# A graph layer kernel on Trainium2: preparation steps divided, edge counts moved beside the keys, two phases given other groups

## The chip, the cores and the metric

The kernel runs on one core of a Trainium2 chip. The metric is the time of one execution on the device in microseconds (us). The engines of the core are named as in the profile: PE (TensorE, matmuls; PEld is its weight load), DVE (VectorE), ACT (ScalarE), POOL (GpSimd) and SP (SyncE, which here issues nearly all DMAs). Each engine works through its own instructions in their order and waits for other engines by semaphores.

## The reference, cut to what matters

There are 32 independent graphs (B) of 512 nodes (N) with 128 features (D). One entry in sixteen of the adjacency matrix, and its diagonal, is not zero.

```python
# layer 0
adj = adj + eye(N)
d = adj.sum(axis=2) ** -0.5
x = layernorm(x + (d[:, :, None] * adj * d[:, None, :]) @ (x @ w0) + b0)
# layer 1, once for each pair (i, j)
pre = (x @ W1[:D])[:, None, :, :] + (x @ W1[D:])[:, :, None, :] + b1
msg = gelu(layernorm(pre, g1, be1))
agg = einsum("bijo,bij->bio", msg, adjacency)
updated = layernorm(concatenate([x, agg]) @ W2 + b2, g2, be2)
x = layernorm(x + updated)
```

The messages of layer 1 cost most. The kernel computes them only for pairs that are edges.

## The kernel before

**Slots and groups.** The 512 nodes of a graph lie in four chunks of 128 (C = 4). For each of the 16 pairs of chunks, the kernel makes a list of the edges of each node: eight slots with the first eight edges, one extra slot for the diagonal pairs of chunks, and two slots of "shared places" for what is left of crowded pairs. A slot has four groups (one for each chunk of receivers), the extra slot has one, so a graph has 8 x 4 + 1 + 2 x 4 = 41 groups, numbered 0 to 40: groups 0 to 31 are the eight slots, 32 is the extra slot (slot 8), 33 to 40 are the shared ones (slots 9 and 10). Over 32 graphs there are 1312 groups.

**The main loop** (in `sparse_path`) runs over the groups in order. One iteration n does this:

- `fetch` (for a slot that begins soon): `gathered`, five groups ahead, reads the slot's list of node numbers from DRAM, spread to all partitions (`raw`, L677). `gathers`, three groups ahead, makes a one-hot matrix of it on DVE (`s`, L687) and has SP transpose it by DMA (`mt`, L689). `deviations` reads three rows per term of the standard deviations (`sd_rows`, L705).
- `pairs(n)` on PE: 16 bf16 matmuls (L724, L725) into a PSUM tile `u`, which has three buffers. In the shared slots, four f32 matmuls (L720) come first; these need `sj` and `ac`, not the one-hot.
- `pass_on`: `aggregate(n-3)` on PE (L772), `sums(n-1)` on DVE (`u_sb`, L734, not in shared slots), `weights(n-1)` on POOL (`sw`, four buffers, L749), `messages(n-2)` on ACT (`m`, L763).
- one step of `finish` of the previous graph, if it is open: the last matmul (`pu`), `u` with its bias (L641), two normalizations, the output.
- `prepare(n)`: some steps of the work that makes ready a later graph or the later slots of this one.

**The preparation** is written as generators. Each `yield` ends a step. The table `plan` gives for each phase the number of steps, and from which group to which (relative to group 0 of its graph) they are spread evenly. So `layer0` of the next graph runs beside groups 0 to 21 of this one, `lists` and `parts` beside 22 to 32, `factors` beside 33 to 37, `more` from group 31 to group 7 of its own graph, and `shared` beside groups 8 to 27.

What these phases do, as far as it is touched here:

- `layer0`: loads `xs` and `a_nat` (1 MB), transposes the adjacency on PE into four banks (L249), and for each bank ACT sums a row (`copied` with `accum_out=deg`, L260) and copies the bank to `a_t` (L261). One DVE instruction makes `mask` (L263) of all four. ACT counts the edges by four sums over `mask` (`counted`, L293). POOL makes the inverse root of the degrees and `xb`. ACT makes `s` and `own_s` (L297, L302). PE multiplies (`pconv`, L311, two halves), DVE makes `y` (L318), a normalization gives `x1` (L208), and PE and ACT turn it (`x1t`, L328). Then `pat`, `pct`, squares and sums on PE and ACT, and at last the `key`s: for each of four q, a matmul `pv` (L365) and two DVE instructions (L361, L362) that read `mask`.
- `lists`: 16 times the eight largest keys and their places on DVE (L399, L400), which ACT casts (`idx_h`, L404), PE turns (`pidx`, L408) and SP writes to DRAM (`idx_d`).
- `more`: 32 steps of three DVE instructions (L455, L457, L458): take out the eight found, find the next eight, and their places. They write into spare columns of `a_t`.
- `shared`: a block of five DVE instructions (L469 to L479), a small count over partitions (`count_h`, `po`, `first`), 16 DVE comparisons (`ended`, L512), eight matmuls and comparisons (`pj` L526, `sj` L522), 16 pairs of matmuls with a copy by ACT (`pl` L537, `sent` L533), the choice of the node numbers in two halves (`chosen`, `picked`, L553, L561), then casts, matmuls and the writes of the extra and shared lists to DRAM (`idx_ds` from `idx_rs`, L582, L386; `sd_ds`). Slots 8, 9 and 10 read those lists.

**Order.** For ACT, POOL and DVE the main loop is under `manual_schedule`: their instructions stand as the code issues them. PE's and SP's instructions are put in order by the framework's planner, which uses its own estimates. Pools with one buffer (`raw` of a width, `mask`, `a_nat`) make a later writer wait for the last reader of what was there.

Of the kernel before, what the change touches and what calls it, by code (L numbers as in the profile page):

```python
# [8 lines left out]
F32 = mybir.dt.float32  # L9
BF16 = mybir.dt.bfloat16  # L10
I32 = mybir.dt.int32
U32 = mybir.dt.uint32
AF = mybir.ActivationFunctionType
ALU = mybir.AluOpType
# [4 lines left out]
P = 128  # L19
# [8 lines left out]
def bcast(ap, n):  # L28

    return ap.unsqueeze(1).to_broadcast([ap.shape[0], n, ap.shape[-1]])  # L30
# [16 lines left out]
def sparse_path(ctx, tc, x, adj, w0, b0, w1, b1, g1, be1, w2, b2, g2, be2, out, most):  # L47
# [21 lines left out]
    nc = tc.nc  # L69
    B, N, D = x.shape  # L70
    C = N // P
# [3 lines left out]
    node = ctx.enter_context(tc.tile_pool(name="node", bufs=1))  # L75
# [67 lines left out]
    rows = {}  # L143
# [72 lines left out]
    def transposed(src, key):  # L216

        pt = bank(f"pt_{key}")
        for c in range(C):
            nc.tensor.transpose(pt[:, c * P : (c + 1) * P], src[:, c, :], ident)  # L220
        return pt
# [3 lines left out]
    def pause(n):  # L225

        for _ in range(n):
            yield

    def layer0(b):  # L230
# [11 lines left out]
        st["edges"] = edges  # L242
        deg = small.tile([P, C], F32, tag="deg", name=f"deg_{b}")
        mask = big.tile([P, C, N], BF16, tag="mask", name=f"mask_{b}")
        px = transposed(xs, f"x_{b}")
        for mc in range(C):
            pt = bank(f"pa_{b}_{mc}")
            for c in range(C):
                nc.tensor.transpose(  # L249
                    pt[:, c * P : (c + 1) * P], a_nat[:, c, mc * P : (mc + 1) * P], ident  # L250
                )
            if mc == 2:
                psup = bank(f"psup_{b}")
                for c in range(C):
                    nc.tensor.matmul(
                        psup[:, c * P : (c + 1) * P], x_t[:, c * P : (c + 1) * P], w0_sb, start=True, stop=True
                    )
            yield
            copied = small.tile([P, N], BF16, tag="copied", name=f"copied_{b}_{mc}", bufs=1)
            nc.scalar.activation(copied, a_nat[:, mc, :], AF.Copy, accum_out=deg[:, mc : mc + 1])  # L260
            nc.scalar.copy(a_t[:, mc, :, :P], pt.rearrange("p (c i) -> p c i", i=P))  # L261
            if mc == C - 1:
                nc.vector.tensor_scalar(  # L263
                    mask.rearrange("p q (c i) -> p (q c) i", i=P),
                    a_t.rearrange("p q c w -> p (q c) w")[:, :, :P],
                    0.0,
                    1.0,
                    ALU.is_equal,
                    ALU.subtract,
                )  # L270
            if mc == 0:
                x_t = node.tile([P, N], F32, tag="t0", name=f"x_t_{b}")
                nc.scalar.copy(x_t, px)
        yield from pause(2)

        deg1 = small.tile([P, C], F32, tag="deg1", name=f"deg1_{b}")
        nc.gpsimd.tensor_scalar(deg1, deg, 1.0, None, ALU.add)
# [7 lines left out]
        nc.gpsimd.tensor_sub(dinv, rdeg, none)  # L285
        dinv2 = small.tile([P, C], F32, tag="dinv2", name=f"dinv2_{b}", bufs=1)
        nc.gpsimd.tensor_tensor(dinv2, dinv, dinv, ALU.mult)
        xb = node.tile([P, C, D], F32, tag="t2", name=f"xb_{b}")
        nc.gpsimd.tensor_tensor(xb, xs, bcast(rows["b0"], C), ALU.add)

        for q in range(C):
            copied = small.tile([P, N], BF16, tag="copied", name=f"counted_{b}_{q}", bufs=1)
            nc.scalar.activation(copied, mask[:, q, :], AF.Copy, accum_out=edges[:, q : q + 1])  # L293

        s = node.tile([P, C, D], F32, tag="t1", name=f"s_{b}")
        for c in range(C):
# [11 lines left out]
        for c in range(C):  # L308
# [4 lines left out]
                )  # L313
            if c % 2:
                yield
        y = node.tile([P, C, D], F32, tag="t3", name=f"y_{b}")
        for c in range(C):
            nc.vector.scalar_tensor_tensor(  # L318
                y[:, c, :], pt[:, c * P : (c + 1) * P], dinv[:, c : c + 1], xb[:, c, :], ALU.mult, ALU.add
            )  # L320
        x1 = node.tile([P, C, D], F32, tag="x1", name=f"x1_{b}", bufs=3)
        yield from layernorm(y, x1, f"l0_{b}")
        st["x1"] = x1
# [33 lines left out]
        key = big.tile([P, C, N], F32, tag="key", name=f"key_{b}")  # L357
        for q in range(C + 1):
            if q:
                here = key[:, q - 1, :]  # L360
                nc.vector.scalar_tensor_tensor(here, pt, a_sum[:, q - 1 : q], c_sum, ALU.add, ALU.add)  # L361
                nc.vector.scalar_tensor_tensor(here, here, -TINY, mask[:, q - 1, :], ALU.min, ALU.mult)  # L362
            if q < C:
                pt = bank(f"pv_{b}_{q}")
                nc.tensor.matmul(pt, at2[:, q * P : (q + 1) * P], ct, start=True, stop=True)  # L365
            yield
# [94 lines left out]
    def shared(b):  # L461
# [7 lines left out]
        nc.vector.scalar_tensor_tensor(over, var, 0.0, sharing, ALU.is_gt, ALU.mult)  # L469
        count = small.tile([P, C * C], F32, tag="count", name=f"count_{b}", bufs=1)  # L470
        nc.vector.tensor_reduce(count, over, AX.X, ALU.add)

        here = small.tile([P, C * C, SLOTS], F32, tag="here", name=f"here_{b}", bufs=1)
        nc.vector.tensor_scalar(here, st["top"], 0.0, None, ALU.is_gt)
# [56 lines left out]
        for n in range(C * C + 1):  # L531
            if n:
                nc.scalar.copy(sent[:, n - 1], pt[:, : SHARED * WIDE].rearrange("p (k w) -> p k w", w=WIDE))  # L533
            if n < C * C:
                pt = bank(f"pl_{b}_{n}")
                for k in range(SHARED):
                    nc.tensor.matmul(  # L537
                        pt[:, k * WIDE : (k + 1) * WIDE],
                        sj[:, n, k * P : (k + 1) * P],
                        at[:, n, :],  # L540
                        start=True,
                        stop=True,
                    )
            if n % 2:
                yield
        yield from pause(3)

        n_r = SHARED * C * C
        chosen = big.tile([P, 2, SHARED, C * C, MORE], F32, tag="mask", name=f"chosen_{b}")
# [80 lines left out]
    def finish(b):  # L630

        st = state.pop(b)
        aggt = st["aggt"]
        pt = bank(f"pu_{b}")
        for c in range(C):
            o, here = pt[:, c * P : (c + 1) * P], slice(c * P, (c + 1) * P)
            nc.tensor.matmul(o, st["x1t"][:, here], w2_sb[:, 0, :], start=True, stop=False)
            nc.tensor.matmul(o, aggt[:, here], w2_sb[:, 1, :], start=False, stop=True)
        yield
        u = node.tile([P, C, D], F32, tag="f0", name=f"u_{b}")  # L640
        nc.vector.tensor_tensor(u, pt.rearrange("p (c d) -> p c d", d=D), bcast(rows["b2"], C), ALU.add)  # L641
        yield
        un = node.tile([P, C, D], F32, tag="f1", name=f"un_{b}")
        yield from layernorm(u, un, f"l1_{b}")
        nc.gpsimd.tensor_tensor(un, un, bcast(rows["g2"], C), ALU.mult)
        yield
        nc.gpsimd.tensor_tensor(un, un, bcast(rows["be2"], C), ALU.add)
        yield
        nc.gpsimd.tensor_tensor(un, un, st["x1"], ALU.add)
        yield  # L650
        o_sb = node.tile([P, C, D], F32, tag="f0", name=f"o_sb_{b}")
        yield from layernorm(un, o_sb, f"l2_{b}")
        yield
        nc.sync.dma_start(out[b].rearrange("(c p) d -> p c d", p=P), o_sb)
# [129 lines left out]
    def advance(gens, steps=1):  # L784
# [12 lines left out]

    n_groups = len(order)
    plan = [
        (layer0, 26, -n_groups, -19),  # L800
        (lists, 21, -19, -8),
        (parts, 7, -19, -10),
        (factors, 7, -8, -3),
        (more, 33, -10, 8),
        (shared, 45, 8, 28),
    ]
    running = {}

# [337 lines left out]
```

## Time and profile before

| | |
|---|---|
| Median of the runs shown | 4013.91 us (three runs, 4012.98 to 4014.3) |
| The profiled execution | 4011.64 us |
| Its span, first to last instruction | 4009.9 us |
| Mean granted clock of PE | 0.985 |
| DMA packets, bytes | 902107, 419.99 MB (105 GB/s in the mean) |
| PE's two largest groups | L772 agg, 1495.7 us; L724 u, 1433.9 us |
| DVE's largest | L734 u_sb, 713.4 us in 1056; L687 s, 421.5 us in 352 |
| ACT's largest | L763 m, 1294.0 us and 288.3 us |
| POOL's largest | L749 sw, 1216.8 us and 296.4 us |

The busy time of an engine is that in which at least one of its instructions is at work. A matmul of f32 operands is shown as two instructions. The number behind "x" is a count, that in brackets at the end of a timeline row is the idle time before, with what ended it. A timeline's columns are: start in us from the span's start, length in us, engine, line, operation, output <- inputs, shapes, count.

### The profile page before, as it was taken

The numbers are of one execution on the slowest core, as the hardware profiler recorded it, in microseconds if no ns is written. First come the engines' busy times: TensorE is split into PE (matmuls) and PEld (weight loads), VectorE is DVE, ScalarE is ACT, GpSimd is POOL, SyncE is SP. The second block draws the span as 40 slices with busy tenths as digits, with TensorE's granted clock in tenths as the row PEclk, the third lists the DMA queues.
The fourth block names the chain that finished last, engine by engine and source line by source line (L and its number), as shares of the span: only waits on it lengthen the run. The fifth ranks groups of instructions, "written<-read, shape, count | busy, mean of one in ns | idle before, by whom it ended". The sixth has DMA issues, their size and how long they took to land. (4 is left out here: it accounts for less than half of the span.)

```text
span 4009.9 us, 108439 instructions
## 1 busy us (share of the span) xinstructions
PE 3766.3 (94%) x39744; PEld 3510.3 (88%) x39744; DVE 3263.9 (81%) x10645; ACT 2791.9 (70%) x8321; POOL 2225.5 (55%) x2526
## 2 busy tenths in 40 slices
PE   5999999999999999999999999999999999999997
PEld 5988889888899888898888998888998889888887
DVE  6888888888887888888888888888888888788892
ACT  4777677676776766776767767667767677676664
POOL 4555565555655555655556555556555565555554
PEclk7999999999999999999999999999999999999998
DMA  3444444444444444444444444444444444444442
GB/s 85 107 109 106 114 101 106 107 107 105 113 102 106 108 106 110 106 106 106 107 105 113 102 106 108 106 112 104 106 105 108 105 108 106 108 107 105 98 105 56
DMA packets 902107, 419.99 MB, mean 105 GB/s; under 512 B 724304, under 2 KB 882192, under 8 KB 901568
## 3 DMA queue, kind: packets, MB, share of 16 engines
q1 hardware_dynamic: 901344, 412.52, 44.1%
q8 instruction: 317, 5.19, 0.5%
q14 instruction: 222, 1.82, 0.1%
q0 software_dynamic: 224, 0.46, 0.1%
HBM read 227.15 MB, written 13.76 MB: 60 GB/s over the span
## 5 line engine op out<-in xcount | busy, mean ns | idle before, releaser
L749 POOL TENSOR_TENSOR sw<-mt,a_t 128x512 f32<-128x512 bf16 x1056 | 1216.8, 1164 | 918.1 <-PE agg L772 764.0
L772 PE MATMUL agg<-sw,m 128*128 128x128 f32 x10496 | 1495.7, 285 | 76.2 <-POOL sw L749 46.1
L724 PE MATMUL u<-c,s 128*128 128x128 bf16 x15744 | 1433.9, 220 | 84.0 <-DVE u_sb L734 80.3
L763 ACT ACTIVATE m<-u_sb,r 128x128 f32<-128x128 f32 x4096 | 1294.0, 395 | 142.3 <-DVE u_sb L734 57.8
L772 PEld LDWEIGHTS agg<-sw,m 128*128 128x128 f32 x10496 | 1304.5, 192 | 94.2 <-POOL sw L749 51.3
L724 PEld LDWEIGHTS <-s 128*128 128x128 bf16 x15744 | 1191.2, 98 | 115.0 <-issue 40.9
L725 PE MATMUL u<-be,sd_rows 128*128 128x128 bf16 x5248 | 1148.6, 220 | 20.7 <-DMA sd_rows<-sd_ds 14.6
L734 DVE TENSOR_TENSOR u_sb<-u,ac 128x512 f32<-128x512 f32 x1056 | 713.4, 676 | 200.6 <-PE u L725 177.1
L725 PEld LDWEIGHTS <-sd_rows 128*128 128x128 bf16 x5248 | 512.7, 98 | 30.7 <-issue 20.0
L763 ACT ACTIVATE m<-u,r_s 128x128 f32<-128x128 f32 x1024 | 288.3, 363 | 251.6 <-PE agg L772 247.4
L533 ACT COPY sent<-pl 128x352 f32<-128x352 f32 x512 | 228.9, 447 | 315.9 <-PE pl L537 278.8
L687 DVE TENSOR_SCALAR s<-raw,node_p 128x2052 bf16<-128x2052 bf16 (+1 forms) x352 | 421.5, 1197 | 20.6 <-DMA raw<-idx_ds 11.9
L720 PE MATMUL u<-ac,sj 128*128 128x128 f32 x2048 | 437.8, 296 | 0.0
L749 POOL TENSOR_TENSOR sw<-mt,sent 128x512 f32<-128x512 bf16 x256 | 296.4, 1163 | 229.0 <-PE agg L772 176.2
L537 PEld LDWEIGHTS pl<-a_t,sj 128*128 128x128 f32 x2048 | 316.2, 191 | 60.7 <-issue 59.2
L457 DVE MAX8 a_t<-key 128x8 f32<-128x128 f32 x1024 | 301.2, 294 | 34.5
L537 PE MATMUL pl<-a_t,sj 128*128 128x176 f32 x2048 | 327.4, 313 | 1.3 <-POOL a_t L505 1.3
L522 DVE TENSOR_SCALAR sj<-pj,node_p 128x512 f32<-128x512 f32 x256 | 187.7, 745 | 153.8 <-PE pj L526 153.8
L720 PEld LDWEIGHTS u<-ac,sj 128*128 128x128 f32 x2048 | 310.0, 192 | 0.4
L458 DVE FIND_INDEX8 idx_m<-a_t,key 128x8 uint32<-128x128 f32 x1024 | 291.4, 285 | 0.0
L311 PEld LDWEIGHTS pconv<-s,a_t 128*128 128x128 f32 x1024 | 141.3, 214 | 57.1 <-ACT s L297 55.4
L361 DVE SCALAR_TENSOR_TENSOR key<-pv,a_sum,c_sum 128x512 f32<-128x512 f32 x128 | 95.7, 748 | 108.3 <-PE pv L365 108.3
(178 smaller groups left out, 4788.8 us busy)
## 6 DMA issues: line engine op xcount, KB each, us to landing
raw<-idx_d SPq DMA_DIRECT2D x256, 513.0 KB
raw<-idx_ds SPq DMA_DIRECT2D x64, 513.0 KB
a_nat<-in_adj_dram SPq DMA_DIRECT2D x32, 1024.0 KB
sd_rows<-sd_d SPq DMA_DIRECT2D x768, 12.0 KB
xs<-in_x_dram SPq DMA_DIRECT2D x32, 256.0 KB
out_dram<-o_sb SPq DMA_DIRECT2D x32, 256.0 KB
mt<-s SPq DMA_TRANSPOSE x352
raw<-idx_ds SPq DMA_DIRECT2D x32, 129.0 KB
```

Source lines behind the costliest of these rows:

```text
L457: nc.vector.max(found, k)
L458: nc.vector.max_index(idx[:, n, h : h + 8], found, k)
L533: nc.scalar.copy(sent[:, n - 1], pt[:, : SHARED * WIDE].rearrange("p (k w) -> p k w", w=WIDE))
L537: nc.tensor.matmul(pt[:, k * WIDE : (k + 1) * WIDE], sj[:, n, k * P : (k + 1) * P], at[:, n, :], start=True, stop=True,)
L687: nc.vector.tensor_scalar(s.rearrange("p (k e) -> p k e", k=3), raw, node_p, None, ALU.is_equal)
L720: nc.tensor.matmul(pu[:, c, :], place, state[b]["ac"][:, q, 0, :], start=first, stop=False)
L724: nc.tensor.matmul(pu[:, c, :], here, c3[:, k, c, :], start=(first and k == 0), stop=False)
L725: nc.tensor.matmul(pu[:, c, :], dev[:, q, c, :], be9, start=False, stop=(c == C - 1))
L734: nc.vector.tensor_tensor(u, pu, a if t == EXTRA else bcast(a[:, q, :], C), ALU.add)
L749: nc.gpsimd.tensor_tensor(sw, mt[:, 0] if t == EXTRA else mt[:, :, q, :], a, ALU.mult)
L763: nc.scalar.activation(m[:, c, :], u[:, c, :], AF.Gelu, scale=r[:, k : k + 1])
L772: nc.tensor.matmul(st["agg"][:, c, :], m[:, c, :], sw[:, c, :], start=(begin and c == 0), stop=(end and c == C - 1),)
```

## The change

It has seven parts.

1. `mask` is made in four quarters (`masked(q)`): quarter mc-1 behind ACT's copy of bank mc, the last one a step later.
2. `xb` is issued a step earlier. The former pause of two steps becomes two steps that do something, with a third behind the degrees.
3. The four counts of edges leave the middle of `layer0`. Each now stands ahead of the two key instructions of its q.
4. `y` is made in two halves, each behind its half of `pconv`, and the normalization begins a step later. `layer0` has 28 steps instead of 26 over the same groups.
5. In `finish` two pauses of a step become pauses of two steps.
6. `more` is spread over 21 groups instead of 18 (to group 10).
7. `shared` has 54 steps instead of 45 and runs beside groups 11 to 27 instead of 8 to 27: its first DVE block is divided by a `yield`, and each copy `sent` with its pair of `pl` matmuls has a step of its own instead of every two; the pause behind it is two steps instead of three.

The planner's order of PE and SP changes with it. On SP, the writes of `idx_ds` stood ahead of the transpose of slot 7 and now stand behind it; the list of slot 9 is now read ahead of that of slot 8. On PE, the first half of `pconv` stood inside `pairs(9)`, ahead of `aggregate(5)`, and now stands behind `aggregate(5)` and ahead of `pairs(9)`. `psd` and three of the four transposes of a later `xs` now stand ahead of the matmuls of slot 9 that need its one-hot.

```diff
@@ -242,6 +242,12 @@
         st["edges"] = edges
         deg = small.tile([P, C], F32, tag="deg", name=f"deg_{b}")
         mask = big.tile([P, C, N], BF16, tag="mask", name=f"mask_{b}")
+
+        def masked(q):
+            nc.vector.tensor_scalar(
+                mask[:, q, :].rearrange("p (c i) -> p c i", i=P), a_t[:, q, :, :P], 0.0, 1.0, ALU.is_equal, ALU.subtract
+            )
+
         px = transposed(xs, f"x_{b}")
         for mc in range(C):
             pt = bank(f"pa_{b}_{mc}")
@@ -259,19 +265,16 @@
             copied = small.tile([P, N], BF16, tag="copied", name=f"copied_{b}_{mc}", bufs=1)
             nc.scalar.activation(copied, a_nat[:, mc, :], AF.Copy, accum_out=deg[:, mc : mc + 1])
             nc.scalar.copy(a_t[:, mc, :, :P], pt.rearrange("p (c i) -> p c i", i=P))
-            if mc == C - 1:
-                nc.vector.tensor_scalar(
-                    mask.rearrange("p q (c i) -> p (q c) i", i=P),
-                    a_t.rearrange("p q c w -> p (q c) w")[:, :, :P],
-                    0.0,
-                    1.0,
-                    ALU.is_equal,
-                    ALU.subtract,
-                )
+            if mc:
+                masked(mc - 1)
             if mc == 0:
                 x_t = node.tile([P, N], F32, tag="t0", name=f"x_t_{b}")
                 nc.scalar.copy(x_t, px)
-        yield from pause(2)
+        yield
+        masked(C - 1)
+        xb = node.tile([P, C, D], F32, tag="t2", name=f"xb_{b}")
+        nc.gpsimd.tensor_tensor(xb, xs, bcast(rows["b0"], C), ALU.add)
+        yield
 
         deg1 = small.tile([P, C], F32, tag="deg1", name=f"deg1_{b}")
         nc.gpsimd.tensor_scalar(deg1, deg, 1.0, None, ALU.add)
@@ -285,12 +288,7 @@
         nc.gpsimd.tensor_sub(dinv, rdeg, none)
         dinv2 = small.tile([P, C], F32, tag="dinv2", name=f"dinv2_{b}", bufs=1)
         nc.gpsimd.tensor_tensor(dinv2, dinv, dinv, ALU.mult)
-        xb = node.tile([P, C, D], F32, tag="t2", name=f"xb_{b}")
-        nc.gpsimd.tensor_tensor(xb, xs, bcast(rows["b0"], C), ALU.add)
-
-        for q in range(C):
-            copied = small.tile([P, N], BF16, tag="copied", name=f"counted_{b}_{q}", bufs=1)
-            nc.scalar.activation(copied, mask[:, q, :], AF.Copy, accum_out=edges[:, q : q + 1])
+        yield
 
         s = node.tile([P, C, D], F32, tag="t1", name=f"s_{b}")
         for c in range(C):
@@ -313,11 +311,13 @@
                 )
             if c % 2:
                 yield
-        y = node.tile([P, C, D], F32, tag="t3", name=f"y_{b}")
-        for c in range(C):
-            nc.vector.scalar_tensor_tensor(
-                y[:, c, :], pt[:, c * P : (c + 1) * P], dinv[:, c : c + 1], xb[:, c, :], ALU.mult, ALU.add
-            )
+                if c == 1:
+                    y = node.tile([P, C, D], F32, tag="t3", name=f"y_{b}")
+                for k in (c - 1, c):
+                    nc.vector.scalar_tensor_tensor(
+                        y[:, k, :], pt[:, k * P : (k + 1) * P], dinv[:, k : k + 1], xb[:, k, :], ALU.mult, ALU.add
+                    )
+        yield
         x1 = node.tile([P, C, D], F32, tag="x1", name=f"x1_{b}", bufs=3)
         yield from layernorm(y, x1, f"l0_{b}")
         st["x1"] = x1
@@ -357,6 +357,9 @@
         key = big.tile([P, C, N], F32, tag="key", name=f"key_{b}")
         for q in range(C + 1):
             if q:
+
+                copied = small.tile([P, N], BF16, tag="copied", name=f"counted_{b}_{q}", bufs=1)
+                nc.scalar.activation(copied, mask[:, q - 1, :], AF.Copy, accum_out=edges[:, q - 1 : q])
                 here = key[:, q - 1, :]
                 nc.vector.scalar_tensor_tensor(here, pt, a_sum[:, q - 1 : q], c_sum, ALU.add, ALU.add)
                 nc.vector.scalar_tensor_tensor(here, here, -TINY, mask[:, q - 1, :], ALU.min, ALU.mult)
@@ -469,6 +472,7 @@
         nc.vector.scalar_tensor_tensor(over, var, 0.0, sharing, ALU.is_gt, ALU.mult)
         count = small.tile([P, C * C], F32, tag="count", name=f"count_{b}", bufs=1)
         nc.vector.tensor_reduce(count, over, AX.X, ALU.add)
+        yield
 
         here = small.tile([P, C * C, SLOTS], F32, tag="here", name=f"here_{b}", bufs=1)
         nc.vector.tensor_scalar(here, st["top"], 0.0, None, ALU.is_gt)
@@ -541,9 +545,8 @@
                         start=True,
                         stop=True,
                     )
-            if n % 2:
-                yield
-        yield from pause(3)
+            yield
+        yield from pause(2)
 
         n_r = SHARED * C * C
         chosen = big.tile([P, 2, SHARED, C * C, MORE], F32, tag="mask", name=f"chosen_{b}")
@@ -643,9 +646,9 @@
         un = node.tile([P, C, D], F32, tag="f1", name=f"un_{b}")
         yield from layernorm(u, un, f"l1_{b}")
         nc.gpsimd.tensor_tensor(un, un, bcast(rows["g2"], C), ALU.mult)
-        yield
+        yield from pause(2)
         nc.gpsimd.tensor_tensor(un, un, bcast(rows["be2"], C), ALU.add)
-        yield
+        yield from pause(2)
         nc.gpsimd.tensor_tensor(un, un, st["x1"], ALU.add)
         yield
         o_sb = node.tile([P, C, D], F32, tag="f0", name=f"o_sb_{b}")
@@ -797,12 +800,12 @@
 
     n_groups = len(order)
     plan = [
-        (layer0, 26, -n_groups, -19),
+        (layer0, 28, -n_groups, -19),
         (lists, 21, -19, -8),
         (parts, 7, -19, -10),
         (factors, 7, -8, -3),
-        (more, 33, -10, 8),
-        (shared, 45, 8, 28),
+        (more, 33, -10, 11),
+        (shared, 54, 11, 28),
     ]
     running = {}
```

## The prediction

> **What bounds the kernel now.** I read the engine shares first, then the stretches of one batch, then the waits, then timelines of the stretches in which TensorE (PE) stands. The page says that PE has work almost all the time:
>
> ```profile
> PE 3766.3 (94%) x39744; PEld 3510.3 (88%) x39744; DVE 3263.9 (81%) x10645; ACT 2791.9 (70%) x8321; POOL 2225.5 (55%) x2526
> ```
>
> Line 781, which ends a batch, first starts at 190.5 us and last at 3987.0 us, so one batch takes (3987.0-190.5)/31 = **122.47 us**. What a change is worth is therefore a matter of the few microseconds per batch in which PE stands. The stretches of one batch (from the 2029.9 us at which line 781 starts; columns: length, then busy us of PE, PEld, DVE, ACT, POOL, granted clock, DMA share, GB/s):
>
> ```profile
> 2029.90:2037.10 7.20, 7.18 (x79) 6.92 (x79) 4.98 (x24) 7.19 (x22) 2.55 (x3) 1.00 0.25 81
> 2037.10:2051.80 14.70, 12.36 (x127) 11.86 (x126) 14.18 (x45) 14.14 (x47) 14.12 (x18) 0.88 0.37 93
> 2051.80:2067.00 15.20, 13.65 (x161) 13.18 (x161) 14.25 (x49) 10.05 (x32) 10.98 (x19) 1.00 0.59 108
> 2067.00:2099.70 32.70, 32.69 (x286) 27.99 (x284) 19.67 (x30) 20.36 (x59) 11.51 (x11) 1.00 0.44 124
> 2099.70:2123.70 24.00, 23.29 (x273) 21.89 (x272) 22.54 (x80) 20.17 (x61) 16.57 (x18) 1.00 0.46 84
> ```
>
> PE is idle 2.3 us in the second stretch and 1.5 us in the third, where VectorE (DVE), ScalarE (ACT) and, for the first of them, GpSimd (POOL) are full. The fourth is PE's alone. In the fifth DVE is again at 94%. The waits name the same places:
>
> ```profile
> PE u L724 <- DVE u_sb L734: 80.3, 69, 2.2
> PE agg L772 <- POOL sw L749: 46.1, 30, 1.6
> PE pidx L408 <- ACT idx_h L404: 15.4, 15, 5.1
> ```
>
> I write pairs(n), sums(n), weights(n), messages(n) and aggregate(n) for the work of group n. Iteration n of the loop issues pairs(n), aggregate(n-3), sums(n-1), weights(n-1), messages(n-2), then the preparation. Three buffers of `u` let PE run at most so far that pairs(n) waits for sums(n-3). Times below are on the clock of that batch.
>
> **Edits that cost nothing by themselves.** The counts of edges (four of L293, 3.00 us on ACT), `xb`, `y` and the steps of `more` keep their number. DVE's sum for a batch grows only by the division of the mask: whole, it takes 1.13 us from start to next start (2040.36 to 2041.49). Four quarters cost at least 1.13 us and at most 4 x 0.61 (the start-to-start of L362, also 128x512) = 2.44 us. I take 4 x 0.35 = 1.4 us, near the lower end, because a quarter of 1.13 is 0.28 and only a start is added. Steps of `more` (replace, max, find) are 0.98 us each.
>
> **Second and third stretch: what is gained.** The counts leave ACT's block of iteration 6, which was messages 1.2 + `un` 1.5 + counts 3.0 + `s` 1.0 + `own_s` 1.0 = 7.7 us and held up `s` and the next messages to 2048.07. They go to iterations 18 to 21, where PE has 3.6 to 5.3 us per iteration and ACT then 3.3 to 3.6: hidden. If PE's rate there fell to the plain 1.84 us per group, they would cost 0.75 us each. On DVE, `more` over 21 groups takes 2 to 3 us out of iterations 1 to 8, and the 3.5 us block of L469 to L479 moves from iteration 8 to 11.
>
> **What is late next: the early quarters of the mask.** In the changed order two of them stand in iteration 3 directly behind `u` of `finish`, ahead of two steps of `more`. The second reads the block of `a_t` that ACT copies in that same iteration:
>
> ```profile
> 2032.42 0.69 DVE L641 TENSOR_TENSOR u<-pu,b_row 128x512 f32<-128x512 f32 x1 [2.05 <-PE pu L638]
> ```
> ```profile
> 2034.92 0.57 ACT L261 COPY a_t<-pa 128x512 f32<-128x512 f32 x1
> ```
> ```profile
> 2040.36 1.22 DVE L263 TENSOR_SCALAR mask<-a_t 128x2048 bf16<-128x2048 f32 x1
> 2059.32 0.68 DVE L734 TENSOR_TENSOR u_sb<-u,ac 128x512 f32<-128x512 f32 x1
> ```
>
> DVE would be there at 2032.42+0.61+0.35 = 2033.4. ACT has been busy without a gap since 2029.91 and ends that copy at 2035.5. So DVE gets a **new wait of 2.1 us**, with all later sums queued behind it. The whole mask never waited at 2040.36. From 2035.5 I add what the changed order gives DVE: rest of iteration 3 2.32, then 2.96, 4.10, 1.58, 2.57, 1.58, 4.27, 3.14, 4.13 for iterations 4 to 11, and sums(11) 0.60: 27.25 us, ending at 2062.8. Before, sums(11) (the last line above) ended at 2060.0. Pairs(14) waits for it. Before, PE did pairs(14) at 2063.4 and then stood for `sw` until 2065.97; now pairs(14) starts at 2062.8 and messages(11) allow aggregate(11) to end by 2064.9, 2.0 us earlier. Of that, three `pj` matmuls not yet done (0.65) come back. So does a new wait: o_sb's normalization (four of L208, 1.55) moves to iteration 14 ahead of the copy `x1t`, so that ACT has messages 1.2 + 1.55 + 0.47 before PE may start `pat`: about 1.2 us. The sum is 2.0-0.65-1.2 = **+0.15 us gained, practically nothing**. The second half of `pconv` now waits for DVE's first `y` (about 0.5 us at 2053), which the wait of pairs(14) covers.
>
> At this place a rule speaks for the change: the Trainium skill, Perfetto Trace Analysis, section Optimizing Scalar/DVE Operations, says that where DVE isn't full but causes bubbles elsewhere, breaking instructions up may let work finish sooner. By it I would leave out the 2.1 us and get a gain of about 1.5 us per batch (pairs(14) at 2061, still behind the x1t wait). The row decides: DVE is at 14.18 of 14.70 us there, and the piece's input is late.
>
> **Fourth stretch.** The same 32 `pl` matmuls and copies, one bank per step instead of two, with PE full as before: zero. If ACT's copies (0.44 us) could no longer follow PE, each iteration would lose some 0.5 us. ACT's 3.3 us against PE's 4.4 says no.
>
> **Fifth stretch: the list of the shared places reaches DVE later.** SyncE's queue (SP) and DVE before:
>
> ```profile
> 2103.82 0.26 SPq L386 DMA_DIRECT2D idx_ds<-idx_rs  x1
> 2104.14 0.24 SPq L387 DMA_DIRECT2D idx_ds<-idx_rs  x1
> 2107.20 2.96 SPq L689 DMA_TRANSPOSE mt<-s  x1
> 2110.26 1.05 SPq L677 DMA_DIRECT2D raw<-idx_ds  x2
> ```
> ```profile
> 2105.86 1.26 DVE L687 TENSOR_SCALAR s<-raw,node_p 128x2052 bf16<-128x2052 bf16 x1
> 2115.13 0.48 DVE L687 TENSOR_SCALAR s<-raw,node_p 128x516 bf16<-128x516 bf16 x1 [0.66 <-DMA raw<-idx_ds]
> ```
>
> Call X the start of the one-hot of slot 7 (2105.86). DVE then has 8.6 us to the one-hot of slot 8, the narrow one. Its list arrives just in time: the narrow `raw` needs 4.8 us from issue to use here, and L687 waits for it 13 times, 11.9 us in all. Now both halves of `chosen` stand in iteration 24, `idx_rs` one iteration later, and on SP its write to DRAM stands **behind** the transpose of slot 7, with the wide list issued **before** the narrow one. The transpose's issue starts at X+1.35 and takes some 2.0 us in most batches, so `idx_ds` goes out at X+3.4 to X+4.0. Behind the transpose's packets it lands at X+5.5. In the prologue, where nothing is in front, the list read followed its write by 0.8 us (53.87 to 54.65). The wide read goes out then, the narrow one at about X+6.3, and its packets trail the wide one's 513 KB: X+11.7. DVE arrives at X+8.6 and waits **3.1 us**. The bounds are 0 (it lands in time) and 5 us (2.96 us for the transpose, 2 us to land). Before, the wait was 0.4 on average. `chosen` moves X itself by +0.5.
>
> The Trainium skill's page DMA: Bandwidth & Descriptors, section on the chain of events of a DMA, gives about 2.0 us plus bytes over 436 GB/s. The narrow list (129 KB) would then take 2.3 us instead of the 4.8 us of the row, `idx_ds` 2.0 us, and the list would be there at about X+8.9: a wait of 0.3 instead of 3.1 us, some 87 us less over 31 batches. I take the row, which contains the queueing behind the transpose.
>
> Behind that instruction DVE holds sums(28), the last lists and so `idx_h`; PE has only 0.6 us of slack at pairs(31) (2116.8 against 2116.2) and waits for `idx_h` already. So PE gets 3.1+0.5-0.4 = 3.2 us. PE's new order gives some back: three of four transposes of the next `xs` (0.67 us) stand in this gap, and DVE's lighter iteration 33 (one step of `more` less, 0.98) brings slot 10's one-hot earlier, worth 0.4 of PE's wait for `sd_rows`. But `psd` now stands ahead of the rest of slot 9: -0.4 us. That is 3.2-0.67-0.4+0.4 = 2.5 us lost.
>
> **Sum.** Per batch -0.15+2.5 = 2.35, plus 0.1 for the quarters that no idle time takes: 2.45 us. Over 31 batches 76 us. The prologue and the end are not on a changed path. The profiled execution took 4011.64 us around a span of 4009.9; the median of the runs shown is 2.3 us higher, so 4013.9+76 = **4090 us**.
>
> **Rivals.** (1) *The relief stays and the list lands in time*: the quick landing of the page and no wait at the quarter leave 1.5 us gained per batch, 4014-47 = 3967. For it: SP's 0.8 us in the prologue, PE's 3.9 us idle. Against: L687 waits already. It decides if the narrow list lands before X+9. (2) *The two cancel*: a list wait near 1.2 us, 4014. (3) *Dearer*: transposes of 2.96 us, a wait of 5 us and a `psd` order that adds a full microsecond give 4.5 us per batch, 4153. (4) *Half*: only 1 us per batch, 4045. (5) That the change does not move what it says: excluded, the changed order shows the counts beside the keys.
>
> **Chances.** Forecast and its surroundings (4060 to 4125) 0.56, half (4022 to 4060) 0.16, dearer 0.08, cancel 0.06, faster 0.14. 0.2% (8 us) is about what this kernel's measurement tells from none. Slower 0.80, same 0.06, faster 0.14. The range 4005 to 4135 leaves out most of the faster and dearer cases; the likeliest case's own is 4060 to 4125.
>
> **What would show it.** Right: DVE waiting at the mask for ACT's `a_t` copy, about 2 us 32 times (60 us); DVE's L690 waiting for `raw<-idx_ds` near 3 us each time (90 us); PE's wait for `idx_h` grown; its wait for `sw` gone; ACT's 3 us block gone. Wrong: L690 waiting under 1 us, or PE's idle between line 781 and `pat` shorter by over 1.5 us. Then the time falls below 4014.

## The result, and the profile after

The changed kernel takes **4106.88 us** in the median of four runs (4102.93 to 4110.38), the kernel before 4013.69 us in the same comparison (4012.98 to 4014.3). The ratio is **1.0232**, with a 95% interval of 1.0214 to 1.025: slower by 93 us. The profiled execution took 4110.38 us around a span of 4108.5.

The page's engine shares show first that no engine has more to do:

```profile
PE 3777.5 (92%) x39744; PEld 3504.6 (85%) x39744; DVE 3235.2 (79%) x10741; ACT 2777.9 (68%) x8321; POOL 2213.7 (54%) x2526
```

PE is busy 11 us longer than before, DVE 29 us less and ACT 14 us less. So most of the loss is time in which PE stands: the span less PE's busy time is 331.0 us here and was 243.6. The line that ends a batch (L784; lines of the late part have moved on by three) starts first at 195.6 us and last at 4085.6: (4085.6-195.6)/31 = 125.48 us per batch, 3.0 more than before.

The stretches of the batch that starts at 2081.44, and the whole batch last (columns as in the prediction's table; the borders follow the work, not the clock):

```profile
2081.44:2116.20 34.76, 30.50 (x357) 29.43 (x356) 29.08 (x113) 25.80 (x81) 25.00 (x32) 1.00 0.34 84
2116.20:2152.80 36.60, 35.43 (x317) 30.48 (x316) 26.95 (x58) 25.98 (x76) 14.80 (x17) 1.00 0.51 125
2152.80:2182.30 29.50, 25.57 (x283) 23.60 (x282) 24.23 (x80) 23.73 (x65) 17.24 (x18) 1.00 0.42 86
2182.30:2207.77 25.47, 25.47 (x296) 25.11 (x295) 20.57 (x88) 11.22 (x40) 11.70 (x11) 1.00 0.58 114
2081.44:2207.77 126.33, 116.97 (x1244) 108.62 (x1243) 100.83 (x336) 86.73 (x260) 68.74 (x78) 1.00 0.46 103
```

PE is idle 4.3 us in the first of these and 1.2 us in the second (the wait for `x1t`), where it was idle 3.9 us in the first four stretches before, and 3.9 us in the third, where it was idle 0.7 us in the fifth. The waits of PE (us in total, times, longest) say at what:

```profile
PE u L727 <- DVE u_sb L737: 97.8, 91, 2.4
PE pidx L411 <- ACT idx_h L407: 52.1, 33, 5.1
PE pconv L309 <- DVE y L317: 46.8, 32, 2.5
PE pat L333 <- ACT x1t L328: 28.3, 31, 1.2
PE psd L435 <- ACT sd L426: 24.1, 31, 2.4
```

The wait of `agg` for `sw` (46.1 us before) is gone. `pidx` stood 15.4 us and `psd` 2.4; those for `y` and `x1t` are new in this size. Behind them are two waits of DVE, the first two of these rows (the last row is from the kernel before):

```profile
DVE s L690 <- DMA raw<-idx_ds: 101.3, 33, 5.1
...
DVE mask L247 <- ACT a_t L267: 67.4, 31, 5.0
DVE s L690 <- DMA raw<-idx_d: 58.8, 48, 2.9
```
```profile
DVE s L687 <- DMA raw<-idx_ds: 11.9, 13, 4.1
```

The first was 11.9 us, the second wasn't there. Each is at one place in every batch. The third, for the lists of the first eight slots, was 6.5 us before. It lies at several places, and it is still 50.6 us in the fastest run below (e11), so it isn't what the loss depends on. Here is the mask in the timeline of that batch, DVE's rows, and then ACT's:

```profile
2083.95 0.69 DVE L644 TENSOR_TENSOR u<-pu,b_row 128x512 f32<-128x512 f32 x1 [2.46 <-PE pu L641]
2084.55 0.42 DVE L247 TENSOR_SCALAR mask<-a_t 128x512 bf16<-128x512 f32 x1
2087.06 0.43 DVE L247 TENSOR_SCALAR mask<-a_t 128x512 bf16<-128x512 f32 x1 [2.08 <-ACT a_t L267]
```
```profile
2086.45 0.58 ACT L267 COPY a_t<-pa 128x512 f32<-128x512 f32 x1
```

DVE stands 2.08 us at the second quarter until ACT has copied its block. And here is the list, SP's rows, then ACT's, then DVE's:

```profile
2158.52 2.93 SPq L692 DMA_TRANSPOSE mt<-s  x1
2161.50 0.49 SPq L389 DMA_DIRECT2D idx_ds<-idx_rs  x1
2162.05 0.24 SPq L390 DMA_DIRECT2D idx_ds<-idx_rs  x1
2163.84 0.92 SPq L680 DMA_DIRECT2D raw<-idx_ds  x2
```
```profile
2157.75 0.57 ACT L585 CAST idx_rs<-pidx_s 9x512 bf16<-9x512 f32 x1
```
```profile
2157.18 1.27 DVE L690 TENSOR_SCALAR s<-raw,node_p 128x2052 bf16<-128x2052 bf16 x1
2169.53 0.48 DVE L690 TENSOR_SCALAR s<-raw,node_p 128x516 bf16<-128x516 bf16 x1 [3.73 <-DMA raw<-idx_ds]
```

With X = 2157.18, the one-hot of slot 7, the list is ready in `idx_rs` at X+1.1, the transposition occupies SP's queue from X+1.3 to X+4.3, the list is written at X+4.3, the two reads (the wide one first) are issued from X+6.7, DVE is ready at X+8.6 and starts the narrow one-hot at X+12.35. This transposition is a long one. In the median of the 32 batches the list is ready at X+1.1, the transposition ends and the write begins at X+3.3, the narrow read is issued at X+6.3, and the narrow one-hot starts at X+11.5. In the kernel before, the medians were: ready at X-2.1, written at once, narrow read first and issued at X+3.4, one-hot at X+8.7.

### The profile page after: what moved, and what is told of

It is laid out like the page before. It is cut to its first block, busy times and chain, and to the rows that moved or that the text cites. A ratio compares the mean times of both kernels' runs of the same rounds, so it can differ in the third digit from the quotient of the medians.

```text
span 4108.5 us, 108258 instructions
## 1 busy us (share of the span) xinstructions
PE 3777.5 (92%) x39744; PEld 3504.6 (85%) x39744; DVE 3235.2 (79%) x10741; ACT 2777.9 (68%) x8321; POOL 2213.7 (54%) x2526
## 5 line engine op out<-in xcount | busy, mean ns | idle before, releaser
L727 PE MATMUL u<-c,s 128*128 128x128 bf16 x15744 | 1418.0, 220 | 101.4 <-DVE u_sb L737 97.8
L690 DVE TENSOR_SCALAR s<-raw,node_p 128x2052 bf16<-128x2052 bf16 (+1 forms) x352 | 422.3, 1200 | 196.0 <-DMA raw<-idx_ds 101.3
L309 PE MATMUL pconv<-s,a_t 128*128 128x128 f32 x1024 | 137.9, 292 | 51.6 <-DVE y L317 46.8
```

The lines of the kernel that those rows point to most:

```text
L690: nc.vector.tensor_scalar(s.rearrange("p (k e) -> p k e", k=3), raw, node_p, None, ALU.is_equal)
L727: nc.tensor.matmul(pu[:, c, :], here, c3[:, k, c, :], start=(first and k == 0), stop=False)
```

## The experiments

The theory after the result: two losses, one at the mask's quarters, one at the list, add up and outweigh a gain of about 1.5 us per batch from the other edits. The rivals are these: the new halves of `y` are the loss (their wait is the third in PE's table); one half of the change, the preparation of layer 0 or the phases, carries all of it; the list is late because of SP's queue and not because its phase ends late. The kernel before was measured with each set of runs: 4011.06 us in the median for the first four, 4013.33 for the next four, 4013.49 for the last four. Their results stand in one table. The last two columns are of the profiled run alone: PE's busy time and the rest of the span, in which PE stands, and the mean granted clock. The profile models the ends of matmuls, so the split is rougher than the span.

| run | median us (lowest to highest) | ratio to before, interval | PE busy / stands, us | clock |
|---|---|---|---|---|
| the kernel before | 4013.69 (4012.98 to 4014.3) | | 3766.3 / 243.6 | 0.985 |
| the changed kernel | 4106.88 (4102.93 to 4110.38) | 1.0232, 1.0214 to 1.025 | 3777.5 / 331.0 | 0.988 |
| mask whole (e1) | 4040.71 (4038.78 to 4043.81) | 1.0072, 1.0055 to 1.0089 | 3787.2 / 254.9 | 0.985 |
| old phases (e2) | 4109.17 (4103.51 to 4113.3) | 1.0246, 1.0228 to 1.0263 | 3806.1 / 298.2 | 0.975 |
| new phases alone (e3) | 4095.81 (4093.11 to 4100.64) | 1.0215, 1.0198 to 1.0232 | 3805.6 / 285.8 | 0.982 |
| moved counts alone (e4) | 4021.19 (4017.3 to 4021.81) | 1.0021, 1.0012 to 1.003 | 3787.4 / 229.4 | 0.978 |
| y whole (e5) | 4103.93 (4102.19 to 4106.26) | 1.0223, 1.0206 to 1.024 | 3766.6 / 337.7 | 0.991 |
| mask and y whole (e6) | 4041.51 (4035.72 to 4042.11) | 1.0065, 1.0048 to 1.0082 | 3767.8 / 272.2 | 0.990 |
| list written by ACT (e7) | 4100.17 (4095.71 to 4103.27) | 1.0212, 1.0195 to 1.0229 | 3781.8 / 318.8 | 0.990 |
| e6 and list by ACT (e10) | 4038.01 (4036.39 to 4041.13) | 1.0059, 1.0042 to 1.0076 | 3778.2 / 261.2 | 0.988 |
| e6 and early list (e11) | **3959.42** (3956.51 to 3960.69) | 0.9868, 0.9852 to 0.9884 | 3747.4 / 207.3 | 0.990 |
| early list (e12) | 4032.99 (4032.13 to 4034.82) | 1.005, 1.0033 to 1.0066 | 3766.4 / 266.7 | 0.990 |
| new phases alone, early list (e13) | 4017.44 (4013.97 to 4022.86) | 1.0012, 1.0005 to 1.0019 | 3790.7 / 223.0 | 0.983 |
| e11, counts back (e14) | 3985.04 (3983.29 to 3991.95) | 0.9935, 0.9918 to 0.9952 | 3768.1 / 215.2 | 0.990 |

**e1, the mask whole.** Against the changed kernel:

```diff
-            if mc:
-                masked(mc - 1)
...
-        masked(C - 1)
+        nc.vector.tensor_scalar(
+            mask.rearrange("p q (c i) -> p (q c) i", i=P),
+            a_t.rearrange("p q c w -> p (q c) w")[:, :, :P],
...
```

> The changed kernel with the mask made by one instruction again, at the place of the last quarter. My theory (late shared list, and a relief in the second and third stretch that DVE's wait for the early quarters takes back): DVE's wait at the mask of 67 us vanishes, the second half of pconv no longer waits for a late y, PE gains 0.5 to 1.5 us per batch there, about 4065 us (4055 to 4095); DVE's wait for raw<-idx_ds stays near 100 us. Rival, that the divided mask is covered by other waits: 4100 to 4110. Rival, that the mask is the main loss: below 4040.

Measured: 66 us less than the changed kernel, close to the 67.4 us that DVE stood at the quarters. That is a larger gain than expected, outside the range of 4055 to 4095 and 0.7 us short of the rival that makes the mask the main loss. PE's waits in this run:

```profile
PE pconv L309 <- DVE y L317: 59.5, 32, 1.9
PE pidx L411 <- ACT idx_h L407: 51.9, 34, 5.1
PE u L727 <- DVE u_sb L737: 32.6, 55, 2.1
```

The wait for `u_sb` falls by 65 us, while that for `y` grows by 13 and is now the largest. `pidx` is unmoved: the list is another matter.

**e2, the old phases.** The changed kernel with `more` and `shared` as before, so that only layer 0's division, the counts, `y` and the pauses of `finish` are new:

```diff
-        (more, 33, -10, 11),
-        (shared, 54, 11, 28),
+        (more, 33, -10, 8),
+        (shared, 45, 8, 28),
```

(and the steps within `shared` as before).

> The changed kernel with the phases more and shared as before (groups, steps, yields); the divided layer0, the moved counts, the halves of y and the pauses in finish stay. My theory: idx_ds stands ahead of the transpose again, DVE's wait for raw<-idx_ds falls from 101 to about 12 us, PE's waits for idx_h and psd fall to those of before, and the 3.2 us per batch come back: about 4010 us (3980 to 4030). Rival, that the loss comes from the divided layer0 and the moved counts: 4080 or more.

A miss by 99 us, and the rival came true: layer 0's side alone loses as much as the whole change. DVE's waits in this run:

```profile
DVE y L317 <- PE pconv L309: 84.0, 33, 5.1
DVE mask L247 <- ACT a_t L267: 68.0, 31, 5.4
...
DVE s L690 <- DMA raw<-idx_ds: 9.2, 12, 3.3
```

The list is in time again (9.2 us), the mask waits as in the changed kernel, and at `y` DVE and PE now wait for each other: PE's second half of `pconv` stands 81.1 us in 32 waits for the first half's `y`. Of the 94 us by which this profiled run is longer than that of the kernel before, PE stands 55 and is busy for 40 more with the same number of matmuls, at a granted clock of 0.975 instead of 0.985. So with the old phases the divided steps cost more than with the new ones.

**e3, the new phases alone**, on the kernel before (e2 undoes these edits in the changed kernel; here they are made alone).

> The kernel before with only more and shared as in the change. My theory: the wait for raw<-idx_ds of about 100 us and the waits at idx_h and psd are there, 3 us per batch lost in the fifth stretch; the block of counts on ACT stays, DVE is lighter in iterations 1 to 8: 4080 us (4050 to 4120). Rival, that it takes the two halves of the change together to lose: within 15 us of 4014.

As expected, a little to the dear side: 85 us above before. PE's waits:

```profile
PE agg L772 <- ACT m L763: 77.0, 62, 2.0
...
PE pidx L408 <- ACT idx_h L404: 51.2, 33, 5.1
PE psd L432 <- ACT sd L423: 24.1, 31, 2.4
```

`pidx` and `psd` stand as in the changed kernel (52.1 and 24.1), with nothing else of the change there: these two belong to the phases. The two sides lose 98 and 85 us alone and 93 together, so the times don't add up. The table shows where: PE stands 55 and 42 us longer than before in the two, and 87 longer with both, which nearly adds up. It is PE's busy time that doesn't: 40 and 39 us more alone, 11 with both. The clock of 0.975 in e2 goes with that; why PE is busy so much longer in e3, at 0.982, stays open.

**e4, the moved counts alone**, on the kernel before:

```diff
-        for q in range(C):
-            copied = small.tile([P, N], BF16, tag="copied", name=f"counted_{b}_{q}", bufs=1)
-            nc.scalar.activation(copied, mask[:, q, :], AF.Copy, accum_out=edges[:, q : q + 1])
...
+                copied = small.tile([P, N], BF16, tag="copied", name=f"counted_{b}_{q}", bufs=1)
+                nc.scalar.activation(copied, mask[:, q - 1, :], AF.Copy, accum_out=edges[:, q - 1 : q])
```

> The kernel before with only the four counts of edges moved beside the keys. My theory: ACT's block of 7.7 us in iteration 6 falls to 4.7, s and the messages come 3 us earlier, while DVE (13.1 us in iterations 5 to 8) still bounds: 0.5 to 1 us per batch gained, about 3990 us (3975 to 4010). Rival, that DVE and POOL hide all of it: 4014. Rival, that the counts cost beside sent and the keys: above 4020.

A miss: some 10 us slower, at the number of the last rival. PE waits less for `sw` and `u_sb`, but more for `m`:

```profile
PE agg L770 <- ACT m L761: 76.6, 31, 2.5
PE u L722 <- DVE u_sb L732: 50.6, 70, 2.2
PE agg L770 <- POOL sw L747: 15.7, 15, 1.5
```

Before these were 30.0, 80.3 and 46.1: in sum 13.5 us less here, while the time is 10 us more. So these waits don't explain it. PE's busy time does:

```profile
PE 3787.4 (94%) x39744; PEld 3521.1 (88%) x39744; DVE 3260.6 (81%) x10645; ACT 2790.6 (69%) x8321; POOL 2225.0 (55%) x2526
```

PE is busy 21 us longer for the same matmuls and stands 14 us less, which is the 7 us between the two profiled spans. The granted clock is 0.978 in place of 0.985, and in all 11 runs of e4 it lies below all 14 of the kernel before (0.978 to 0.980 against 0.983 to 0.987). The share not granted is 4016.8 x 0.022 = 88 us here and 4009.9 x 0.015 = 60 us before, so the clock is large enough as an explanation. One place where it shows is behind the new wait for `m`:

```profile
2067.24 1.97 PE L770 MATMUL agg<-sw,m 128*128 128x128 f32 x8 [2.48 <-ACT m L761]
```

From 2060 to 2072 us the clock is 0.86. The eight matmuls take 1.97 us here and 1.16 us in the kernel before where it is 1.00 (at 2065.97). That the longer wait brings the lower clock is likely from this, but no run holds the one fixed and changes the other.

**e5, e6: y whole**, with the mask's quarters (e5) and with the mask whole (e6). Against the changed kernel:

```diff
-                if c == 1:
-                    y = node.tile([P, C, D], F32, tag="t3", name=f"y_{b}")
-                for k in (c - 1, c):
-                    nc.vector.scalar_tensor_tensor(
...
+        y = node.tile([P, C, D], F32, tag="t3", name=f"y_{b}")
+        for c in range(C):
+            nc.vector.scalar_tensor_tensor(
```

> The changed kernel with y computed in one piece, after both halves of pconv; the mask's quarters and the new phases stay. If the second half of pconv pays for waiting on the first half's y, its wait in the changed kernel (46.8 us over 32) goes and nothing takes its place: about 4060 us (4045 to 4080). If the quarters of the mask alone set the time of this stretch and y's halves only show where PE was late anyway: 4090 to 4110. If y's halves brought a gain (an earlier x1t): above 4115, with a longer wait of pat for x1t.

> The changed kernel with the mask in one piece and y in one piece; the counts beside the keys, the pauses of the finish and the new phases stay. If the mask's quarters and y's halves are two separate losses, this gains what the whole mask gave (66 us) and the 59.5 us that pconv then waits for y: about 3985 us (3970 to 4005), faster than before, with only the wait of the one-hot for idx_ds (some 3 us per batch) left. If they are one loss seen at two places, it stays where the whole mask alone stood: 4030 to 4045.

Neither gains anything, as the rivals said: 4103.93 against 4106.88 us with ranges that overlap, and 4041.51 against 4040.71. In e5 the wait of `pconv` is gone, and others have taken its place:

```profile
PE u L726 <- DVE u_sb L736: 114.3, 121, 2.1
...
PE po L490 <- ACT count_h L486: 45.7, 32, 1.5
```

`u_sb` stood at 97.8 and `po` at 12.4 in the changed kernel; 16.5+33.3 = 49.8 us come back for the 46.8 that went. The halves of `y` are only the place at which PE, ahead of DVE there, is held first. My theory that they were a loss of their own falls.

**e7, e10: the list written from another queue.** `idx_ds` goes out by ACT's queue, on the changed kernel (e7) and on e6 (e10):

```diff
-        nc.sync.dma_start(rows_d[:n].rearrange("(n j) -> n j", j=N), rows)
-        nc.sync.dma_start(rows_d[n:].unsqueeze(0), rows[:1, :PAD])
+        queue = nc.scalar if tag == "idx_ds" else nc.sync
+        queue.dma_start(rows_d[:n].rearrange("(n j) -> n j", j=N), rows)
+        queue.dma_start(rows_d[n:].unsqueeze(0), rows[:1, :PAD])
```

> The changed kernel with one difference: idx_ds is written to DRAM from ScalarE's queue in place of SyncE's, so the write does not stand behind the transposition of slot 7. The wide read (slot 9) is still issued ahead of the narrow one (slot 8). If the place of the write behind the transposition makes the list late, the wait of the one-hot at L690 for idx_ds falls from 101 us to 50 us or less and the time to about 4065 us (4045 to 4085). If the wide read ahead of the narrow one makes it late, or the phase simply ends too late, the wait stays above 80 us and the time at 4095 to 4110.

> The changed kernel with the mask and y in one piece and idx_ds written from ScalarE's queue. If the three losses are separate, the gains of the two others add: about 3945 us (3930 to 3970), faster than the kernel before by over 1%. If the write's place is not what makes the list late: as with the mask and y in one piece alone, about 3985. If another wait takes the place of the list's: between, with the wait named by PE's waits in the stretch of slots 8 and 9.

Both go the rival's way, with 7 and 4 us gained in ranges that overlap (the 3985 us expected for e10 rested on the first case of e6, which did not come). DVE's wait for the list stays at 99.5 us in e7. In its timeline:

```profile
2157.88 1.27 DVE L691 TENSOR_SCALAR s<-raw,node_p 128x2052 bf16<-128x2052 bf16 x1
2158.45 0.57 ACT L586 CAST idx_rs<-pidx_s 9x512 bf16<-9x512 f32 x1
2159.22 2.74 SPq L693 DMA_TRANSPOSE mt<-s  x1
2160.68 1.28 ACT L767 ACT_TABLE_LOAD   x1
2162.03 0.27 ACTq L390 DMA_DIRECT2D idx_ds<-idx_rs  x1
```

With the transposition out of its way, the write still goes out 4.15 us after the one-hot of slot 7, which is the median too (3.3 in the changed kernel). It stands in ACT's own order two steps behind `idx_rs`, and ACT's instructions in between, this table load among them, hold it for 3.0 us from the end of `idx_rs` at 2159.02. So e7 takes the write from behind one thing and puts it behind another; it doesn't show that SP's queue is harmless. The changed kernel's own rows speak for both causes: the list is ready 3.2 us later than before (X+1.1 against X-2.1), 0.2 us ahead of the transposition's issue, and SP then sends it 2.2 us later in the median.

**e11, e12, e13: the list early.** One number, on e6, on the changed kernel and on e3:

```diff
-        (shared, 54, 11, 28),
+        (shared, 54, 11, 25),
```

> The changed kernel with the mask and y in one piece, and the shared phase over groups 11 to 24 in place of 11 to 27, so that the write of idx_ds is issued ahead of the transposition of slot 7 and some 5 us earlier; the narrow read is then issued ahead of the wide one. If the list was late because its phase ends too late (in the run with the mask and y in one piece the write was issued 8 us before the one-hot of slot 8 could start, and DVE waited 3.7 us), the wait for idx_ds falls from 104 us to under 20 us, PE's waits at pidx and psd (54 and 25 us) to under 20 us together, and the time by 60 to 95 us: about 3960 us (3940 to 3985), faster than before. If the same steps in fewer groups make DVE late between groups 11 and 25 instead: 4010 to 4045, with a longer wait of PE for u_sb.

> The changed kernel with one difference: the shared phase over groups 11 to 24 in place of 11 to 27. The mask's quarters and y's halves stay. If list and mask are separate losses: the same gain as between the two runs with the mask in one piece, about 80 us, so about 4027 us (4010 to 4050), still slower than before. If the denser phase costs DVE its slack where the mask's quarters already stall it: 4060 to 4110.

> The kernel before with only the phases of the change (more over 21 groups, shared in finer steps), and shared over groups 11 to 24. If the list alone made the phases cost 82 us, this is at the time of before or faster: about 4005 us (3975 to 4020). If the phases cost by their other effect (the wait of agg for m, 77 us with the phases alone against 30 us before): 4040 to 4070.

All three lie in the ranges of the theory: the time falls by 82 us on e6 (4041.51 to 3959.42), by 74 on the changed kernel (4106.88 to 4032.99) and by 78 on e3 (4095.81 to 4017.44). e11's timeline, SP's rows and then DVE's:

```profile
2078.58 0.27 SPq L388 DMA_DIRECT2D idx_ds<-idx_rs  x1
2078.90 0.24 SPq L389 DMA_DIRECT2D idx_ds<-idx_rs  x1
2079.99 0.38 SPq L679 DMA_DIRECT2D raw<-idx_ds  x1
2084.79 1.65 SPq L691 DMA_TRANSPOSE mt<-s  x1
2086.53 1.20 SPq L679 DMA_DIRECT2D raw<-idx_ds  x1
```
```profile
2083.46 1.26 DVE L689 TENSOR_SCALAR s<-raw,node_p 128x2052 bf16<-128x2052 bf16 x1
2091.76 0.47 DVE L689 TENSOR_SCALAR s<-raw,node_p 128x516 bf16<-128x516 bf16 x1
```

The write is issued 4.9 us ahead of the one-hot of slot 7, the narrow read alone follows 1.1 us after the second write, and slot 8's one-hot starts at X+8.3 without a wait. In e12 DVE's wait for the list is all but gone:

```profile
DVE s L690 <- DMA raw<-idx_ds: 2.8, 1, 2.8
```

In the three kernels PE stands 65, 64 and 63 us less than without the early list, 2.1 us per batch; the rest is busy time. The one number also puts the narrow read ahead of the wide one again. In the changed kernel the narrow read is issued 0.5 us behind the wide one, and no run takes the two apart. In e11 PE's waits for `pidx` are down to 8.2 us; its largest are now

```profile
PE po L490 <- ACT count_h L486: 52.6, 32, 1.7
PE pj L529 <- DVE sj L525: 35.8, 58, 1.2
PE u L726 <- DVE u_sb L736: 33.6, 72, 2.7
```

The denser phase costs some `pj` waits (35.8 us) and still leaves the largest gain of these runs. This is a version that **beats both kernels**: 54 us, 1.3%, under the kernel before.

**e14, the counts back** where they were, the rest as e11 (the reverse of e4's edit).

> As the run with the mask and y in one piece and the early list, but the edges are counted where they were before, in one block after dinv, not beside the keys. If the moved counts cost what they cost alone (10 us): some 10 us faster than that run. If they gain there, because ScalarE's block of 3 us delays m: 10 to 60 us slower. If they are hidden at both places: within 4 us of it.

It is 26 us slower than e11: the moved counts, which cost 10 us alone, gain 26 here. The reason that was expected isn't seen, since `agg` waits for `m` in neither table. In e14's table

```profile
PE u L727 <- DVE u_sb L737: 80.0, 102, 2.7
...
PE po L491 <- ACT count_h L487: 8.8, 32, 1.2
```

PE waits 80.0 us for `u_sb` where e11 has 33.6, but only 8.8 for `count_h` where e11 has 52.6. In the profiled run it stands 8 us longer in all. It is also busy for 21 us more, at the same clock of 0.990 and with the same matmuls, and what makes that isn't found. So the moved counts shorten PE's standing in both schedules (14 us in e4, 8 here), and it is PE's busy time that turns the sign.

## Why the prediction was right

The forecast was 4090 us, the time 4106.88: the sign is right, and the loss 93 us instead of 76, 3.0 us per batch instead of 2.45. That the range of 4005 to 4135 held says little, since it contains the time of the kernel before; the narrower 4060 to 4125 held too, and both mechanisms that were to make the loss are there.

**The list**: right, in size and in its reason, and shown. Forecast: write at X+3.4 to 4.0 behind the transposition, narrow read at X+6.3, DVE at X+8.6, list at X+11.7, a wait of 3.1 us, PE losing 2.5. In the median of the batches: X+3.3, X+6.3 and X+11.5, and a wait of 101.3/33 = 3.1 us; with the list early the same kernel gains 74/31 = 2.4 us per batch. The prediction took the row's 4.8 us for the narrow read and not the 2.3 us that it drew from the Trainium skill (DMA: Bandwidth & Descriptors, Anatomy of one DMA — SWDGE (gpsimd) path). It took the better figure: the section fits its 2.0 us plus bytes over 436 GB/s to DMAs issued by GpSimd, and this list is read on SP's queue. Here it is over 5 us from the narrow read's issue to the use at 2169.53, behind the wide read. The term for `psd`, 0.4 us, was 24.1/31 = 0.8.

**The mask's quarters**: right, and shown. Forecast 2.1 us of new wait, 60 us over the run; measured 67.4/31 = 2.2, and whole masks give back 66 us (late list) and, with `y`, 74 us (early list). The rule that breaking instructions up may let work finish sooner (Trainium skill, Perfetto Trace Analysis, Optimizing Scalar/DVE Operations) is said of engines that aren't saturated. The prediction was right not to lean on it: DVE was at 14.18 of 14.70 us there, the piece's input was late, and the pieces cost time.

**The net of the early stretches** is the term that was mis-sized: "+0.15 us gained, practically nothing". With the list out of the way (e12) the change is still 19.5 us slower than before, 0.63 us per batch lost. The relief was there: without quarters (e11) the kernel gains 54/31 = 1.7 us per batch, its denser phase and whole `y` included, and the prediction had named about 1.5 for that case. What it took too small is the price of the quarters to PE: in effect it let 1.5-0.15 = 1.35 us of DVE's 2.1 us of wait reach PE, because `pat` would then wait for `x1t`, and by e12 and e11 they cost 74/31 = 2.4 us, of which PE's standing is 59/31 = 1.9. The waits for `x1t` came, at 28.3/31 = 0.9 us against 1.2.

**The third stretch** was read wrongly in one point: ACT was not full there, but busy 10.05 of 15.20 us; only DVE was. And the clock has no term in the sum, though the second stretch shows 0.88. Between these two kernels that matters little (0.985 and 0.988 over the whole run), but e2 and e4 show that an edit at this place can move it.

**The second half of `pconv`**, "about 0.5 us", covered by the wait of pairs(14): the wait is 46.8/32 = 1.5 us, three times the size, but it is covered, as e5 and e6 show.

**The counts**, costed at nothing, are not nothing: they cost 10 us alone (e4) and gain 26 in e11. What they do in the changed kernel itself wasn't measured. Nor were `xb`'s place, the later normalization and the pauses of `finish` taken apart; what of the 1.7 us each gives stays open. Rival 1, relief that stays with a list in time, at 3967 us, is not what this change does. It takes the mask and `y` whole and the shared phase three groups shorter, and then the time is 3959 us.

## What to carry to other kernels

When a producer's phase is moved or stretched, count backward from its consumer: write, landing, read and queue together took about 8 us here, so a step that ends one or two groups later turns from hidden to a wait in full. Look also at what stands next on the queue: the list was ready 3.2 us later and was written over 5 us later, because a transposition had come in between. Divide a step for an in-order engine only where each piece's input is there when the engine reaches it; otherwise everything behind waits for the earliest piece's late input. Don't add up a wait table as a price list: removing a 47 us wait gave 3 us, while a 67 us wait gave 66, and only a run told them apart. Before a wait is blamed, compare the busiest engine's busy time and its granted clock: in e4 PE stood less and took longer.

## What was unexpected

The list's read followed its second write by 1.1 us in the median of e11, 1.4 in e7, where ACT's queue wrote it, and 1.6 in the changed kernel, where the write stood directly behind a transposition. Whether the transposition's packets cause the difference wasn't tried.
